# Attention over 32 graphs: transposed probabilities go between partition quadrants through a scratch tensor in HBM

## The chip, the cores and the metric

The kernel runs on one core of one Trainium2 chip. The metric is the device time of one execution in microseconds (us), the median of several runs. A core has five engines with their own instruction streams: PE (matrix multiplications; its weight loads are shown apart, as PEld), DVE (vector), ACT (scalar functions), POOL and SP. In this kernel SP does nothing but issue DMA transfers.

## The reference, cut to what matters

There are 32 graphs of 512 nodes with 256 features each (`x`), and a 512 x 512 adjacency matrix each (`adj`). Four layers follow one another, each with a residual and a layer normalization:

```
q, k, v = split_heads(x @ Wq + bq), ...              # 8 heads of 32
scores  = where(adj > 0, q @ k.T / sqrt(32), NEG)
x = layernorm(x + softmax(scores) @ v @ Wo + bo)      # layer 0
x = layernorm(x + relu(((1+eps) x + adj @ x) @ W1 + b1) @ W2 + b2)              # layer 1
x = layernorm(x + silu(rmsnorm((eps x + adj @ x) @ W1 + b1)) @ W2 + b2)         # layer 2
x = layernorm(x + softplus(xn @ W_self + (I - normalized adj) @ xn @ W_neigh))  # layer 3
```

All of it is in 32-bit floating point. The graphs are independent of each other.

## The kernel before, in words

The function `graph(b)` records the operations of one graph; nothing is issued while it runs. Each recorded operation has one or more ways, and a way names an engine, a cost in nanoseconds and the code that issues it. When all 32 graphs are recorded, `Order.emit` plays the operations through a list scheduler and issues them in the order it finds. Every engine takes, among the operations that can start within 100 ns of the earliest, the one with the lowest due time. The due time of an operation is the graph's number times `PERIOD`, plus its place in its own graph (a mix of earliest and latest, weighted by `LATE`), plus a shift for its stage from the table `LEAD`; the last graph is brought forward by `HASTE`. The scheduler also knows the number of buffers of each tile, a cost `TURN` for changing the shape in which PE's array is used[...]. So work of several graphs is interleaved, and costs, shifts and period decide the order on every engine.

Attention (`attend(g)`) works on groups of four heads and on row tiles of 128 nodes: 2 groups x 4 row tiles, eight row tiles per graph, 256 in all. For one row tile:

1. PE computes scores for four heads into the four banks of `sc` (L715, four passes side by side, each on 32 rows of the array).
2. DVE adds the mask `bias`, takes the row maximum and writes to `pq`, once per head (L734). ACT takes the exponential in place (L748).
3. DVE transposes `pq` in place (L761). Its transpose works within blocks of 32 x 32, so afterwards blocks sit in the wrong group of 32 partitions (a quadrant).
4. Sixteen DMA moves carry each 32-partition block of `pq` to its place in `pT` (L773), 64 KB each. In the first graph the moves of a tile are four operations, which the scheduler may give to SP's or ACT's queue; in the other graphs all sixteen are one operation on SP.
5. PE multiplies the values with two row tiles of `pT` into `po_att` (L815, four passes side by side, each on 32 columns of the array).

There are two `pq` buffers and three `pT` buffers. PSUM has four banks for `sc` and four more (tag `m`) that all other matrix products take turns in: `pq` of the projections (L643), `pv` (L684), `pm_t` and `pr_r` of the softmax denominators (L862, L875), `po` (L902), `ph` (L1077), `pa` and `pg` (L1094), `pm` and `pb` of the root mean square (L1180, L1210), `pt` (L1270), `pz` (L1298) and `pa_l` (L1340). The copy from `pr_r` to `oT` is at L526, the step that empties a `pz` bank into `zy` is at L1309, its scaling at L1325 or L1319. The loads of `adjT` and `xT`, in rows of 128 bytes, are at L565; `adj` and `x` have loads of their own (L390, L387).

Of the kernel before, what the change touches and what calls it, by code (L numbers as in the profile page):

```python
# [9 lines left out]
F32 = mybir.dt.float32  # L10
# [9 lines left out]
RMS_EPS = 1e-6  # L20
HEADS = 8

PERIOD = 73742
LEAD = {
    "adjT": 6800, "agg1": 6800, "agg2": -35400, "degree": -29100, "diag": -31500,
    "lap": -106500, "ln0": -12800, "ln1": -36800, "ln2": 4400, "ln3": 118000, "load": 57500,
    "move": -2300, "pv": -3300, "pz": 12100, "qk": 46700, "rinv": -33100, "rms": -12600,
    "scores": -3500, "silu": -120800, "softplus": -44300, "v": 78100, "w11": -39800,
    "w12": -64200, "w21": -29300, "w22": 4400, "wo": -14600, "x3T": -44400, "xT": -7800,
}  # L30


# [27 lines left out]
class Order:  # L60
# [8 lines left out]
    WAIT = 70  # L69
    TABLE, TABLE_DUE = 1300, 9000  # L70

    TURN = {"whole": 93, "row": 180, "col": 93}
    TURN_DUE = 4000
    LATE = 0.97
    HASTE = 53985

    def __init__(self):
        self.ops = []
# [29 lines left out]
    def run(self, ops, key, back=False):  # L108
# [20 lines left out]
        slots = {}  # L129
        cand = {e: [] for e in self.LAT}  # L130
        table, turn = [None], ["whole"]
        pool_busy = [0.0, 0.0]

        def add(o):
            for i, way in enumerate(o.ways):
# [18 lines left out]
        while len(out) < len(ops):  # L154
            best = None
            for e, lst in cand.items():
                if not lst:
                    continue
                opts = []
                for c in lst:  # L160
                    o = c[2]
                    st = slot_time(o)
                    if st is None:
                        continue
                    t = max(free[e], o.ready, st)
                    way = o.ways[c[3]]
                    if e == "DVE" and "port" in way[3] and pool_busy[0] <= t < pool_busy[1]:
                        t = pool_busy[1]
                    k = c[0]
                    tb = way[3].get("table")  # L170
                    if tb and tb != table[0]:
                        k += self.TABLE_DUE
                    if e == "PE" and way[3].get("turn", "whole") != turn[0]:
                        k += self.TURN_DUE
                    if len(o.ways) > 1:
                        f0 = t + way[1]
                        worse = False
                        for j, other in enumerate(o.ways):
                            if j != c[3] and max(free[other[0]], o.ready) + other[1] < f0 - 1:
                                worse = True  # L180
                        if worse:
# [26 lines left out]
            if e == "PE":  # L208
                tu = way[3].get("turn", "whole")
                if tu != turn[0]:  # L210
                    cost += self.TURN[tu]
                    turn[0] = tu
            if e == "POOL" and cost > 500:
                pool_busy[:] = [t, t + cost]
            for way2 in o.ways:
                lst = cand[way2[0]]
                for i in range(len(lst) - 1, -1, -1):
                    if lst[i][2] is o:
                        del lst[i]
            o.t0, o.t1, o.way = t, t + cost, way  # L220
            free[e] = o.t1 - self.TAIL[e] if e != "SP" else t + way[3].get("issue", 100)
            end = o.t1 + way[3].get("lat", self.LAT[e])
            for x in o.bufs:
                if not x.taken:
                    x.taken = True
                    s = slots[x.slot]
                    s.remove(min(s))
# [50 lines left out]
def kernel(  # L278
# [40 lines left out]

    const = ctx.enter_context(tc.tile_pool(name="const", bufs=1))  # L320
    sb = ctx.enter_context(tc.tile_pool(name="sb", bufs=2))
    ps = ctx.enter_context(tc.tile_pool(name="ps", bufs=1, space=PSUM))


# [168 lines left out]
    def graph(b):  # L493
# [74 lines left out]
        d_out, d_in = small("d_out"), small("d_in")  # L568
        for q in range(4):
            op(  # L570
                [("SP", 1650, lambda q=q: load_blocks(adjT(), adj[b], q), {"issue": 1650, "lat": 6000})],
                [], [(adjT, m, q) for m in range(NT)],
            )
        for m0 in range(0, NT, 2):
# [31 lines left out]
        xT = tmp([P, DC, N], "xT", 1)  # L606
        for q in range(4):
            op(
                [("SP", 800, lambda q=q: load_blocks(xT(), x[b], q), {"issue": 800, "lat": 4000})],
                [], [(xT, c, q) for c in range(DC)],  # L610
            )
        dve(
# [87 lines left out]
        def attend(g):  # L700
# [6 lines left out]
            for t in range(NT):  # L707
# [59 lines left out]
                pT = tmp([P, 4, HPG, NT, 32], "pT", 3)  # L767
                pTs.append(pT)

                def move(queue, to, pq=pq, pT=pT):  # L770
                    for a in to:
                        for i in range(4):
                            queue.dma_start(  # L773
                                pT[32 * a : 32 * a + 32, i], pq[32 * i : 32 * i + 32, a]
                            )

                pqk = [(pq, j) for j in range(HPG)]
                if first:

                    for a in range(4):  # L780
                        op(
                            [
                                (
                                    "SP", 2230,
                                    lambda a=a, move=move: move(nc.sync, [a]),
                                    {"issue": 2230},
                                ),
                                (
                                    "ACT", 2400,
                                    lambda a=a, move=move: move(nc.scalar, [a]),  # L790
                                    {"lat": 2000},
                                ),
                            ],
                            pqk, [(pT, a)],
                        )
                else:
                    op(
                        [(
                            "SP", 8900, lambda move=move: move(nc.sync, range(4)),
                            {"issue": 8900},  # L800
                        )],
                        pqk, [(pT, a) for a in range(4)],
                    )

                if t % 2 == 0:
                    continue
# [3 lines left out]
                def pv(two=two):  # L810
# [10 lines left out]
                            )  # L821

                pe(
                    1960, pv,
                    [(pT, a) for _, pT in two for a in range(4)] + [(v, c) for c in range(NT)],
                    [(po,)], oT, turn="col",
                )
# [3 lines left out]
            tj = [(t, j) for t in range(NT) for j in range(HPG)]  # L831
            rv = small("rv", 2, [P, NT, HPG])
            dve(
                170,
                lambda: nc.vector.reciprocal(rv(), rs()),
                [(rs, t, j) for t, j in tj], [(rv,)],
            )
# [2 lines left out]
            for r in range(3):  # L840
                dst = part[:, :, :, r]
                dve(
                    150,
                    lambda dst=dst, left=left: nc.vector.tensor_copy(dst, left()),
                    [(left,)], [("parts", g), ("parts", g, r)], port=True,
                )
                if r < 2:
                    rest = small("rest", 2, [P, NT, HPG])
                    dve(
                        150,  # L850
                        lambda dst=dst, left=left, rest=rest: nc.vector.tensor_tensor(
                            rest(), left(), dst, ALU.subtract
                        ),
# [6 lines left out]
            def tr():  # L860
# [10 lines left out]
            )  # L871
            pr_r = bank("pr_r")
            pe(
                220,
                lambda: nc.tensor.matmul(  # L875
                    pr_r(),
                    lhsT=sel_r.rearrange("p j e -> p (j e)"),
# [415 lines left out]
        for t in range(NT):  # L1293
            pz = bank("pz")

            def mm(t=t, pz=pz):
                for c in range(DC):
# [23 lines left out]
                    ),  # L1321
                ),
                (
                    590,
                    lambda t=t: nc.scalar.activation(  # L1325
                        zy[:, t, D : 2 * D], zy[:, t, D : 2 * D], AF.Identity,
                        scale=s_in[:, t : t + 1],
# [5 lines left out]
        for tp in range(NT // 2):  # L1333
            pa = bank("pa_l")
            for i in range(2):
                t = 2 * tp + i

                def mm(t=t, i=i, pa=pa):
# [6 lines left out]
                            stop=(m == NT - 1),  # L1345
                        )

                pe(1740, mm, allT + [(zy, m, 1) for m in range(NT)], [(pa, i)])
                dve(
                    430,  # L1350
                    lambda t=t, i=i, pa=pa: nc.vector.scalar_tensor_tensor(
                        out=zy[:, t, 0:D],
                        in0=pa[:, i * D : (i + 1) * D],
# [99 lines left out]
```

## Time and profile before

| | |
|---|---|
| median of 3 runs | 3562.94 us (3562.31 to 3564.2) |
| the profiled execution | 3560.7 us, span 3558.9 us |
| mean granted TensorE clock | 0.981 |
| busy share of the span | PE 96%, DVE 79%, PEld 57%, ACT 52%, POOL 24% |
| DMA moves `pT<-pq` | 4048 on SP's queue, 48 on ACT's, 64 KB each, 2.0 us to landing |
| DMA in all | 395.10 MB, 653361 packets |
| HBM | 105.79 MB read, 16.78 MB written |

The profile is that of one execution. The span runs from the first to the last instruction; the execution's own time has a little around it. Busy time of an engine is the time in which one of its instructions was running; for PE, matrix passes overlap and their ends are modelled, so 96% busy does not mean 96% of its peak. The granted clock is the share of full speed that the chip gave PE.

### The profile page before, as it was taken

To read this page: it belongs to the slowest core of one execution; us is meant where nothing else is said; L and a number is where in the kernel's file an instruction comes from. 1 tells how busy PE (TensorE), PEld (TensorE's weight loads), DVE (VectorE), ACT (ScalarE), POOL (GpSimd) and SP (SyncE) were. 2 spreads that over 40 slices of the span, in tenths; PEclk is the share of its full clock that TensorE was granted. 3 is DMA by queue.
4 is the path that set the end of the run, shared out by engine and by line. 5 is a ranking of instruction groups with operands and counts; after the bars stand their busy time and mean duration, and the time that the engine had idled before them with its cause. 6 is when DMAs were issued, how large, how long until landed. Compare 5 with 4: busy or idle time off the path is not lost.

```text
span 3558.9 us, 59695 instructions
## 1 busy us (share of the span) xinstructions
PE 3404.3 (96%) x19848; PEld 2031.2 (57%) x19848; DVE 2817.0 (79%) x6324; ACT 1865.4 (52%) x3797; POOL 863.1 (24%) x614
## 2 busy tenths in 40 slices
PE   5799999999999999999999999999999999999997
PEld 2455655655655655556565556565556556556565
DVE  5778787888787888787888877887887888788865
ACT  2355554465554555555555545555554555554633
POOL 0122222222222222221222221322221222222221
PEclk7999999999999999999999999999999999999998
DMA  6644444444444454444444444444444444444420
GB/s 165 145 118 112 113 116 110 116 118 103 117 118 113 110 118 106 113 110 118 119 114 108 118 107 118 116 116 103 116 112 115 114 110 116 114 113 109 102 51 12
DMA packets 653361, 395.10 MB, mean 111 GB/s; under 512 B 468864, under 2 KB 505088, under 8 KB 653056
## 3 DMA queue, kind: packets, MB, share of 16 engines
q1 hardware_dynamic: 650752, 388.14, 45.9%
q10 hardware_dynamic: 2304, 3.15, 0.4%
q8 instruction: 160, 2.62, 0.3%
q14 instruction: 145, 1.19, 0.1%
HBM read 105.79 MB, written 16.78 MB: 34 GB/s over the span
## 4 chain that ended last, share of the span: by engine, by line
PE 75%; SPq 12%; DMA 5%; DVE 4%; issue 2%; ACT 1%; POOL 0%; DVEq 0%; POOLq 0%; ACTq 0%
PE po L902 13%; PE pg L1094 12%; SPq L773 12%; PE ph L1077 11%; PE pa_l L1340 6%; PE po_att L815 6%; PE sc L715 6%; PE pa L1094 5%; PE pq L643 5%; PE pz L1298 4%; PE pv L684 3%; DMA pT<-pq 3%; DVE pq L734 2%; DMA x<-in_x_dram 1%; PE pm L1180 1%
## 5 line engine op out<-in xcount | busy, mean ns | idle before, releaser
L748 ACT ACTIVATE pq<-pq,mx 128x512 f32<-128x512 f32 x1024 | 727.3, 711 | 610.0 <-DVE mx L734 308.6
L734 DVE CUSTOM_DVE_ANT_0 pq<-sc,bias 128x512 f32<-128x512 f32 x1024 | 658.5, 685 | 235.1 <-DMA pT<-pq 180.7
L761 DVE STREAM_TRANSPOSE pq<-pq 128x2048 f32<-128x2048 f32 x256 | 587.9, 2297 | 85.3 <-ACT pq L748 82.6
L902 PE MATMUL po<-w,gT 128*128 128x256 f32 x2048 | 460.0, 383 | 4.3 <-ACT gT L1233 4.3
L1094 PE MATMUL pg<-hT,w 128*128 128x512 f32 x1024 | 447.8, 596 | 0.0
L955 POOL TENSOR_TENSOR rstd<-ve,nhalf 128x4 f32<-128x4 f32 x132 | 143.5, 1087 | 1226.6 <-DVE ve L950 1052.4
L902 PEld LDWEIGHTS po<-w,gT 128*128 128x128 f32 x2048 | 389.0, 191 | 82.7 <-issue 23.6
L715 PE MATMUL sc<-kT,qT 32*128 32x512 f32 x2048 | 298.9, 653 | 40.1 <-DVE mx L734 26.1
L1094 PEld LDWEIGHTS pg<-hT,w 128*128 128x128 f32 x1024 | 192.4, 190 | 252.1 <-issue 221.2
L1298 PE MATMUL pz<-wsn,xnT 128*128 128x512 f32 x512 | 259.4, 634 | 49.7 <-DVE zy L1309 28.6
L533 POOL TENSOR_TENSOR ssq<-ssq,sq 128x512 f32<-128x512 f32 x219 | 287.4, 1312 | 67.0 <-ACT sq L1170 55.6
L815 PEld LDWEIGHTS po_att<-pT,v 128*32 128x32 f32 x8192 | 224.2, 113 | 110.2 <-issue 60.9
L815 PE MATMUL po_att<-pT,v 128*32 128x128 f32 x8192 | 261.8, 281 | 16.4 <-DMA pT<-pq 12.7
L533 POOL TENSOR_TENSOR sp<-sp,y 128x1024 f32<-128x1024 f32 x31 | 73.0, 2354 | 774.1 <-ACT sp L1390 750.1
L1077 PE MATMUL ph<-adjT,y 128*128 128x512 f32 x512 | 230.6, 593 | 0.0
L1340 PE MATMUL pa_l<-zy,adjT 128*128 128x256 f32 x1024 | 229.1, 381 | 1.2 <-ACT zy L1325 0.9
L1077 PE MATMUL ph<-adjT,y_att 128*128 128x512 f32 x512 | 229.8, 601 | 0.0
L1094 PE MATMUL pa<-hT,w 128*128 128x512 f32 x512 | 228.3, 599 | 0.0
L902 PE MATMUL po<-w,aT 128*128 128x256 f32 x1024 | 226.7, 380 | 0.7 <-DVE aT L1118 0.7
L1340 PEld LDWEIGHTS pa_l<-zy,adjT 128*128 128x128 f32 x1024 | 193.5, 190 | 44.8 <-issue 14.8
L902 PEld LDWEIGHTS po<-w,aT 128*128 128x128 f32 x1024 | 192.4, 190 | 27.1 <-DVE aT L1118 1.7
L1374 ACT ACTIVATE sp<-zy 128x1024 f32<-128x1024 f32 (+1 forms) x33 | 34.0, 1031 | 319.8 <-PE ph L1077 297.7
(136 smaller groups left out, 5101.9 us busy)
## 6 DMA issues: line engine op xcount, KB each, us to landing
pT<-pq SPq DMA_DIRECT2D x4048, 64.0 KB, 2.0
adj<-in_adj_dram SPq DMA_DIRECT2D x32, 1024.0 KB, 5.3
adjT<-in_adj_dram SPq DMA_DIRECT2D x128, 256.0 KB, 4.4
xT<-in_x_dram SPq DMA_DIRECT2D x128, 128.0 KB, 3.7
x<-in_x_dram SPq DMA_DIRECT2D x32, 512.0 KB, 5.4
out_dram<-sp SPq DMA_DIRECT2D x31, 512.0 KB, 3.3
pT<-pq ACTq DMA_DIRECT2D x48, 64.0 KB, 2.2
w<-in_L_gnn_W_dram SPq DMA_DIRECT2D x2, 1024.0 KB, 6.1
```

Source lines behind the costliest of these rows:

```text
L533: lambda: nc.gpsimd.tensor_tensor(dst(), dst(), src(), ALU.add), {},
L715: nc.tensor.matmul(sc[:, j, :], lhsT=qT[hp, g, t * P : (t + 1) * P], rhs=kT[hp, g, :], start=True, stop=True,)
L734: lambda t=t, j=j, sc=sc, row=row: nc.vector.tensor_tensor_reduce(out=row(), in0=sc[:, j, :].rearrange("p (a n) -> p a n", a=4), in1=bias[ ...
L748: lambda t=t, j=j, row=row: nc.scalar.activation(row(), row(), AF.Exp, bias=mx[:, t, j : j + 1], scale=-1.0, accum_out=rs[:, t, j : j + 1],),
L761: lambda pq=pq: nc.vector.transpose(pq().rearrange("p a j c s -> p (a j c s)"), pq().rearrange("p a j c s -> p (a j c s)"),),
L773: queue.dma_start(pT[32 * a : 32 * a + 32, i], pq[32 * i : 32 * i + 32, a])
L815: nc.tensor.matmul(po[j * HD : (j + 1) * HD, t * P : (t + 1) * P], lhsT=v[:, c, h * HD : (h + 1) * HD], rhs=pT[:, :, j, c, :], start=(c == 0),
L902: nc.tensor.matmul(po[:, i * D : (i + 1) * D], lhsT=lhs[:, k, t * P : (t + 1) * P], rhs=w[:, k, :], start=(i == 0 and k == 0), stop=(i == ...
L1077: nc.tensor.matmul(ph(), lhsT=xin[:, m, c * P : (c + 1) * P], rhs=adjT[:, m, :], start=(m == 0), stop=(m == NT - 1),)
L1094: nc.tensor.matmul(pa(), lhsT=w[:, c, m * P : (m + 1) * P], rhs=hT[:, c, :], start=(c == 0), stop=(c == DC - 1),)
L1298: nc.tensor.matmul(pz(), lhsT=xnT[:, c, t * P : (t + 1) * P], rhs=wsn[:, c, :], start=(c == 0), stop=(c == DC - 1),)
L1340: nc.tensor.matmul(pa[:, i * D : (i + 1) * D], lhsT=adjT[:, m, t * P : (t + 1) * P], rhs=zy[:, m, D : 2 * D], start=(m == 0), stop=(m == N ...
```

## The change

The moves between quadrants go through HBM. A new pool `dr` holds a scratch tensor `via` with four buffers. After the transpose, four DMAs write a quadrant of `pq` each (256 KB, all four target quadrants at once); when they have landed, one DMA reads 1 MB into `pT`, where each partition's 8 KB are contiguous. All of them are on SP's queue, for the first graph too.

```diff
+    dr = ctx.enter_context(tc.tile_pool(name="dr", bufs=1, space=bass.MemoryType.DRAM))
...
-                def move(queue, to, pq=pq, pT=pT):
-                    for a in to:
-                        for i in range(4):
-                            queue.dma_start(
-                                pT[32 * a : 32 * a + 32, i], pq[32 * i : 32 * i + 32, a]
-                            )
...
-                    op(
-                        [(
-                            "SP", 8900, lambda move=move: move(nc.sync, range(4)),
-                            {"issue": 8900},
-                        )],
-                        pqk, [(pT, a) for a in range(4)],
-                    )
...
+                via = Buf(dr, [4, 32, 4, HPG * NT * 32], F32, "via", f"via_{b}", 4)
+
+                def away(pq=pq, via=via):
+                    for i in range(4):
+                        nc.sync.dma_start(
+                            via[:, :, i, :].rearrange("a p e -> p a e"),
+                            pq[32 * i : 32 * i + 32].rearrange("p a j c s -> p a (j c s)"),
+                        )
+
+                op(
+                    [("SP", 2240, away, {"issue": 2240, "lat": 4500})],
+                    [(pq, j) for j in range(HPG)], [(via,)],
+                )
+                op(
+                    [(
+                        "SP", 600,
+                        lambda pT=pT, via=via: nc.sync.dma_start(
+                            pT().rearrange("p i j c s -> p (i j c s)"),
+                            via().rearrange("a p i e -> (a p) (i e)"),
+                        ),
+                        {"issue": 600, "lat": 5500},
+                    )],
+                    [(via,)], [(pT, a) for a in range(4)],
+                )
```

The scheduler's numbers change with it: `PERIOD` from 73742 to 71815, every entry of `LEAD`, `TURN` for the row shape from 180 to 200, `TURN_DUE` from 4000 to 4750, `LATE` from 0.97 to 1.14, `HASTE` from 53985 to 24390.[...] Some costs change, among them these:

```diff
-                [("SP", 1650, lambda q=q: load_blocks(adjT(), adj[b], q), {"issue": 1650, "lat": 6000})],
+                [("SP", 1250, lambda q=q: load_blocks(adjT(), adj[b], q), {"issue": 1250, "lat": 4500})],
...
-                    1960, pv,
+                    1780, pv,
...
-                    590,
+                    500,
                     lambda t=t: nc.scalar.activation(
                         zy[:, t, D : 2 * D], zy[:, t, D : 2 * D], AF.Identity,
...
-                    430,
+                    475,
                     lambda t=t, i=i, pa=pa: nc.vector.scalar_tensor_tensor(
                         out=zy[:, t, 0:D],
```

What is computed does not change, and the instructions on PE are the same ones in another order.

More of the change, by code (lines that the diff above doesn't have):

```diff
@@ L21 @@
 HEADS = 8
-PERIOD = 73742
+PERIOD = 71815
 LEAD = {
[L25 to L29, printed above, removed]
+    "adjT": 118100, "agg1": 26800, "agg2": -178200, "degree": 63800, "diag": 700,
+    "lap": -205500, "ln0": -84700, "ln1": -132100, "ln2": -13100, "ln3": 175600, "load": 16100,
+    "move": -135200, "pv": 1100, "pz": -31400, "qk": 19100, "rinv": -44200, "rms": -37100,
+    "scores": -14700, "silu": -127000, "softplus": 8300, "v": 122200, "w11": 17900,
+    "w12": -76100, "w21": 900, "w22": 5000, "wo": -50100, "x3T": -163400, "xT": -19500,
 }
@@ L70 @@
     TABLE, TABLE_DUE = 1300, 9000
[L72 to L75, printed above, removed]
+    TURN = {"whole": 93, "row": 200, "col": 93}
+    TURN_DUE = 4750
+    LATE = 1.14
+    HASTE = 24390
     def __init__(self):
@@ L131, in run @@
         table, turn = [None], ["whole"]
-        pool_busy = [0.0, 0.0]
+        pool_busy, dve_busy = [0.0, 0.0], [0.0, 0.0]
         def add(o):
@@ L168, in run @@
                         t = pool_busy[1]
+                    if e == "POOL" and dve_busy[0] <= t < dve_busy[1]:
+                        t = dve_busy[1]
                     k = c[0]
@@ L212, in run @@
                     turn[0] = tu
-            if e == "POOL" and cost > 500:
+            if e == "POOL" and cost > 1100:
                 pool_busy[:] = [t, t + cost]
+            if e == "DVE" and "port" in way[3]:
+                dve_busy[:] = [t, t + cost]
             for way2 in o.ways:
@@ L608, in graph @@
             op(
-                [("SP", 800, lambda q=q: load_blocks(xT(), x[b], q), {"issue": 800, "lat": 4000})],
+                [("SP", 660, lambda q=q: load_blocks(xT(), x[b], q), {"issue": 660, "lat": 4000})],
                 [], [(xT, c, q) for c in range(DC)],
@@ L768, in attend @@
                 pTs.append(pT)
-                def move(queue, to, pq=pq, pT=pT):
-                    for a in to:
-                        for i in range(4):
-                            queue.dma_start(
-                                pT[32 * a : 32 * a + 32, i], pq[32 * i : 32 * i + 32, a]
-                            )
-                pqk = [(pq, j) for j in range(HPG)]
-                if first:
-                    for a in range(4):
-                        op(
[L782 to L794, printed above, removed]
-                        )
-                else:
-                    op(
-                        [(
-                            "SP", 8900, lambda move=move: move(nc.sync, range(4)),
-                            {"issue": 8900},
-                        )],
-                        pqk, [(pT, a) for a in range(4)],
-                    )
@@ L833, in attend @@
             dve(
-                170,
+                240,
                 lambda: nc.vector.reciprocal(rv(), rs()),
@@ L842, in attend @@
                 dve(
-                    150,
+                    190,
                     lambda dst=dst, left=left: nc.vector.tensor_copy(dst, left()),
@@ L849, in attend @@
                     dve(
-                        150,
+                        180,
                         lambda dst=dst, left=left, rest=rest: nc.vector.tensor_tensor(
@@ L873, in attend @@
             pe(
-                220,
+                130,
                 lambda: nc.tensor.matmul(
@@ L1346, in mm @@
                         )
-                pe(1740, mm, allT + [(zy, m, 1) for m in range(NT)], [(pa, i)])
+                pe(1728, mm, allT + [(zy, m, 1) for m in range(NT)], [(pa, i)])
                 dve(
-                    430,
+                    475,
                     lambda t=t, i=i, pa=pa: nc.vector.scalar_tensor_tensor(
```

## The prediction

> **What bounds the kernel now.** I read the page first, then the stretches, then PE's waits, then DVE's and the DMA issues, then the timeline.
>
> ```profile
> span 3558.9 us, 59695 instructions
> PE 3404.3 (96%) x19848; PEld 2031.2 (57%) x19848; DVE 2817.0 (79%) x6324; ACT 1865.4 (52%) x3797; POOL 863.1 (24%) x614
> ...
> PEclk7999999999999999999999999999999999999998
> ```
>
> PE is the bound: 96% busy, the next engine 79%. No engine but PE can shorten the middle of the run; PE can do so only by idling less, by running less often at a low clock, or by needing fewer changes of array shape. Where its idle time lies is told by four stretches (length, then busy time of PE, PEld, DVE, ACT, POOL, then clock, DMA share, GB/s):
>
> ```profile
> 0.00:120.00 120.00, 63.54 (x439) 33.30 (x440) 75.94 (x163) 38.70 (x102) 9.84 (x13) 0.76 0.72 170
> 120.00:270.00 150.00, 135.57 (x818) 76.05 (x817) 116.13 (x256) 69.32 (x146) 33.88 (x23) 0.97 0.48 120
> 270.00:3330.00 3060.00, 3004.73 (x17663) 1794.55 (x17663) 2486.74 (x5584) 1662.75 (x3396) 776.16 (x543) 0.99 0.48 113
> 3330.00:3559.00 229.00, 200.47 (x933) 127.32 (x931) 138.21 (x325) 94.60 (x154) 43.22 (x35) 0.94 0.20 49
> ```
>
> PE idles 120 - 63.5 = 56 us in the first stretch, 14 in the second, 55 in the long middle, 29 at the end. The start is a third of all idle time in 3% of the span. PE's waits in the middle alone (waiting line, what it waited for, us in total, times, longest):
>
> ```profile
> PE pz L1298 <- DVE zy L1309: 28.6, 9, 3.6
> PE pz L1298 <- ACT oT L526: 20.7, 18, 1.9
> PE sc L715 <- DVE mx L734: 4.0, 10, 1.2
> ```
>
> No line there names a DMA: the 16 moves per row tile are hidden from PE in the middle. They aren't hidden from the engines that feed it; over the whole run:
>
> ```profile
> ACT pq L748 <- DMA pT<-pq: 230.0, 52, 15.0
> DVE pq L734 <- DMA pT<-pq: 180.7, 112, 4.9
> ```
>
> These are reductions and exponentials that can't overwrite a `pq` buffer (two of them) until its 16 moves have landed. Issues (KB each, median us to landing):
>
> ```profile
> pT<-pq SPq DMA_DIRECT2D x4048, 64.0 KB, 2.0
> adj<-in_adj_dram SPq DMA_DIRECT2D x32, 1024.0 KB, 5.3
> ...
> out_dram<-sp SPq DMA_DIRECT2D x31, 512.0 KB, 3.3
> ```
>
> What one change of array shape costs, from the timeline:
>
> ```profile
> 1502.79 3.62 PE L902 MATMUL po<-wo,oT 128*128 128x256 f32 x16
> 1506.24 7.07 PE L902 MATMUL po<-w,gT 128*128 128x256 f32 x32
> 1513.24 1.14 PE L715 MATMUL sc<-kT,qT 32*128 32x512 f32 x8
> 1514.31 7.17 PE L902 MATMUL po<-w,gT 128*128 128x256 f32 x32
> 1521.42 1.14 PE L715 MATMUL sc<-kT,qT 32*128 32x512 f32 x8
> ```
>
> From start to start 16 passes take 3.45 us, so 32 take 6.90; between two score groups they take 7.11. The score group takes 1.07 for two rounds of four passes side by side, 0.86 at 0.43 a pass. The detour adds 0.21 + 0.21 us for two changes: **0.21 us a change**.
>
> **What the Trainium skill says.** "TensorEngine Tiling (Array Packing)", Key Properties: changing the tiling mode drains TensorE; the 0.21 us agree. "TensorE: Matmul & The Clock Gate", Part 1: the clock falls to half after an idle window of about 3.4 us and needs a busy one to recover. The trace agrees: after the 3.6 us wait at 799 us, four `pz` passes take 3.5 us instead of 1.8. So a long stall costs about 1.7 us more than its length; the short ones aren't followed by this. "DMA: Bandwidth & Descriptors", Anatomy of one DMA: a fixed 2 us, mostly the receipt of the write, heaviest for HBM, plus bytes / 436 GB/s. That fit (it is for the gpsimd path) gives an estimate of 2.6 us for 256 KB and 4.4 us for 1 MB; the trace's 512 KB store takes 3.3, its 1 MB load 5.3, slower than the fit.
>
> **The change part by part.**
>
> *SP's issue time.* Before: 16 x 0.589 us (median of L773) = 9.4 us per row tile, 75 us per graph of about 107. After: four writes at the same price and one read at 0.53 (the `adj` load): 2.9 us per tile, 23 per graph. SP wasn't PE's bound, so this alone is worth nothing in the middle.
>
> *Latency of one tile.* Before 9.4 + 2.0 = 11.4 us. After: 4 x 0.589 to issue, a landing W of the last write, 0.5 to issue the read, a landing R. No row shows a 256 KB write to HBM from 32 partitions; W lies between 2.1 us (fastest store to the output) and 3.4 (slowest), I take 2.7. R is a 1 MB load: 4.4 (skill) to 10 (slowest `adj` load), I take 5.3. Sum 2.4 + 2.7 + 0.5 + 5.3 = 10.9 us, 9.4 to 16.3. No gain here; but `pq` is free after 2.4 + 2.7 = **5.1 us instead of 11.4**, and four scratch buffers stand between `pq` and the three `pT`.
>
> *Start.* A `pq` buffer's cycle is 2.7 us of reductions, 0.9 of the last exponential, 2.3 of transpose, then the move: 17.3 us before, 8.7 per tile with two buffers; the first 11 score groups start 10.2 us apart (16.7 to 118.5 us). After, 11.0 / 2 = 5.5. Then DVE is next: its 76 us in the first 120 are about 6.6 per tile. 11 tiles at 8 instead of 10.2 save 24 us. DMA limits it: share 0.72 already, and 12 reads of 1 MB are added at about 3 us of all engines each (358 GB/s below): (0.72 x 120 + 36) = 122 us of DMA work in the same stretch, unless the order spreads it, which it does in part, since weights move later. The first graph also loses ACT's queue for moves. I take **-20 us**, bounds -45 (DVE alone) and +5.
>
> *Order in the middle.* `PERIOD`, `LEAD`, `LATE` and the costs reorder every engine. Several costs come to what the trace shows: L1351 from 430 to 475 (trace 472), L1325 from 590 to 500 (498). In PE's order the four `pz` groups of a graph, split by other shapes before, follow each other behind 6.9 us of `po`, so DVE has emptied `xnT` and their banks by then; and three score groups stand 6.9 us apart, which the old 8.7 us cycle couldn't have fed and 5.5 can. The waits shown are 53 of 55 us idle, plus 9 long ones x 1.7 = 15 us at low clock: 70 us at stake. PE's producers DVE and ACT keep their load (the order moves some 55 `gT` copies from DVE to ACT, and others back). I take **-45 us**, bounds -70 and +10.
>
> *Changes of shape.* Counting PE's order by 128x128, 32-row and 32-column groups: 727 before, 675 after. 52 x 0.21 = **-11 us**.
>
> *New waits.* The read waits on SP for its write to land and for a `pT`; behind it on SP stand the next writes and loads, so a late `po_att` holds them. Four `po_att` groups now stand within some 30 us, around the eight `pg`. With three `pT`, the read of the last of these tiles can start only when the first half of the third group is done; from there to the second half of the fourth PE has 0.9 + 1.1 (`sc`) + 0.9 (`pm`) + 3.5 (`pq`) + 0.9 (`pb`) + 1.0 = **8.3 us** of other work. The read needs 0.5 + 5.3 = 5.8 if the rings are empty. They aren't: in those 30 us, five reads, one or two tiles of writes, an `adj` load and the end of `adjT` want the engines. The `adj` load shows the price of a load with long rows:
>
> ```profile
> 1500.00:1504.00 4.00, 4.00 (x46) 3.47 (x47) 2.92 (x5) 3.83 (x4) 0.00 (x0) 1.00 0.64 229
> ```
>
> 229 GB/s at a share of 0.64 is 358 GB/s in full, 2.9 us per MB; moves alone ran at 103 GB/s for 0.42, 4.3 us per MB. Five reads 15, two tiles 9, `adj` 3: 27 of 30 us. Over the run 256 x 2.9 us add 0.21 to a share of 0.46. I take **+15 us** (0.5 us a graph), bounds 0 and +130.
>
> *End.* The tail after the last `pg` has the same matmuls with little moved: 0, bounds -5 and +5.
>
> Sum: -20 - 45 - 11 + 15 = -61 us. The profiled execution took 3560.7 us (span 3558.9), 2.2 under the median 3562.9, which is nothing against these bounds. Predicted: 3502 us.
>
> **The rivals.** *A, reads late at `po_att`*: for it, 27 of 30 us; against it, no DMA wait of PE in the middle today. If they land 3 us past their slack at two groups a graph, PE waits 2 x 3 us, 31 times: +186, less 76 gained: 3670. It decides from 76 / 31 = 2.5 us of new PE waiting per graph on. *B, start and shape changes alone*: the new order has waits of its own in place of those at `pz` (DVE is 79% busy and in order): -20 - 11 = 3531. *C, both work out*: no stall left in the middle, DVE alone at the start: -45 - 70 - 11: 3436. *D, nothing*: moves were hidden and new waits eat the rest: 3563.
>
> **How the numbers follow.** About 0.2% (7 us) is what a measurement of this kernel can tell from no change. Forecast (3480 to 3520) 0.45, B 0.16, C 0.14, D 0.05 within 0.2%, slower 0.20 (A 0.14, a wait of DVE's in the new order 0.06). Faster 0.75. The range of 8 in 10 leaves out most of A and the lower end of C: 3435 to 3590.
>
> **What would show it.** Right: PE idle in the first 120 us near 35; `pz` gone from PE's waits; DMA waits of L734 and L748 far smaller; DMA share near 0.67; SP's queue mostly idle. Wrong: `po_att` behind `DMA pT<-via` at the top of PE's waits, each graph; a read landing over 8 us; a mean clock below 0.981.

## The result, and the profile after

The change makes the kernel 0.3% faster: **3551.5 us** (median of 17 runs) against 3560.4 us (17 runs), ratio 0.9971, 95% interval 0.9959 to 0.9983. The sign of the forecast was right and its size was not: about 9 us came of 61. The profiled execution took 3558.9 us, at the slow end of its runs, and its span is only 2.3 us shorter than that of before; the gains and losses below are told against the spans.

The heads of the page of after, to set beside those of before:

```profile
span 3556.6 us, 55212 instructions
PE 3393.6 (95%) x19848; PEld 2032.6 (57%) x19848; DVE 2823.1 (79%) x6308; ACT 1900.1 (53%) x3810; POOL 839.8 (24%) x613
```

PE is busy for 10.7 us less, but the span shrank by 2.3 only: idle time grew by 8.4. The same four stretches tell where (length, busy time of PE, PEld, DVE, ACT, POOL, clock, DMA share, GB/s):

```profile
0.00:120.00 120.00, 64.90 (x362) 30.49 (x362) 67.00 (x140) 37.15 (x92) 8.37 (x12) 0.76 0.90 235
120.00:270.00 150.00, 133.78 (x892) 77.98 (x893) 116.97 (x265) 72.44 (x163) 30.82 (x22) 0.95 0.73 224
270.00:3330.00 3060.00, 2990.49 (x17614) 1792.17 (x17616) 2495.21 (x5561) 1696.80 (x3399) 758.75 (x545) 0.99 0.68 190
3330.00:3557.00 227.00, 204.45 (x990) 131.98 (x982) 143.91 (x343) 93.74 (x156) 41.89 (x34) 0.96 0.31 86
```

PE's idle time, before to after: 56.5 to 55.1 us in the first 120 us, 14.4 to 16.2 in the next 150, **55.3 to 69.5 in the middle**, 28.5 to 22.6 at the end. The loss is in the middle. PE's waits there (waiting line, what it waited for, us in total, times, longest):

```profile
PE pb L1207 <- DVE diag L1201: 50.8, 27, 4.4
PE sc L721 <- DVE mx L740: 9.1, 5, 2.1
PE pz L1295 <- DVE y L913: 4.4, 8, 1.7
...
PE po_att L812 <- DMA pT<-via: 0.3, 1, 0.3
```

The waits at `pz` are gone, as forecast (49.3 us before, 4.4 now), and the read of the scratch tensor is never late for `po_att`. But `pb`, the product that spreads the root mean square over the partitions in layer 2, waits once in nearly every graph. No DMA is named, so one has to ask why `diag` was late. The timeline of one graph, on all engines (start, length, engine, line, operation; in brackets the idle time before it and what ended it):

```profile
1382.02 0.38 SPq L396 DMA_DIRECT2D adj<-in_adj_dram  x1
...
1389.15 1.05 PE L1177 MATMUL pm<-ones,ssq 128*128 128x1 f32 x8
...
1390.89 2.29 DVE L1001 TENSOR_REDUCE d_in<-adj 128x4 f32<-128x2048 f32 x1 [2.10 <-DMA adj<-in_adj_dram]
...
1393.10 0.15 DVE L1189 TENSOR_SCALAR ms<-pm 128x4 f32<-128x4 f32 x1
...
1393.33 1.02 POOL L549 TENSOR_TENSOR rr<-ms,nhalf 128x4 f32<-128x4 f32 x1 [5.40 <-DVE ms L1189]
...
1394.38 0.87 DVE L1201 TENSOR_SCALAR diag<-ident,rr 128x128 f32<-128x128 f32 x4
...
1395.40 1.10 PE L1207 MATMUL pb<-diag,ones 128*128 128x512 f32 x2 [1.65 <-DVE diag L1201]
```

Read it from below. `pb` waits for `diag`, `diag` for POOL's `rr`, `rr` for `ms`. The input of `ms`, the sums in `pm`, was ready at 1390.2 while DVE stood still, yet `ms` starts at 1393.1: on DVE it stands behind `d_in`, the row sum of the next graph's adjacency matrix, and here DVE keeps to its order. `d_in` stood still for 2.1 us because its load, issued at 1382.0, took 8.8 us to arrive. Over the whole run:

```profile
DVE pq L740 <- DMA via<-pq: 72.4, 45, 8.4
DVE d_in L1001 <- DMA adj<-in_adj_dram: 70.6, 28, 5.7
```

The first line is the gain that was sought: reductions waited 180.7 us for the moves, now 72.4 for the writes (ACT's exponentials 230.0 before, 3.9 now). The second is new. The DMA issues of the page show why (KB each, median us from issue to landing):

```profile
via<-pq SPq DMA_DIRECT2D x1024, 256.0 KB, 4.4
pT<-via SPq DMA_DIRECT2D x256, 1024.0 KB, 7.6
adj<-in_adj_dram SPq DMA_DIRECT2D x32, 1024.0 KB, 8.8
...
out_dram<-sp SPq DMA_DIRECT2D x31, 512.0 KB, 7.2
```

The load of `adj` takes 8.8 us instead of 5.3, in a middle whose DMA share has gone from 0.48 to 0.68.

That it matters is due to the new order as well. In the kernel before, `d_in` started some 30 us after its load was issued; one graph of it:

```profile
1385.64 0.53 SPq L390 DMA_DIRECT2D adj<-in_adj_dram  x1
...
1416.19 2.27 DVE L1004 TENSOR_REDUCE d_in<-adj 128x4 f32<-128x2048 f32 x1
```

A load of 8.8 us would have been in time there. After the change DVE comes to `d_in` 6.8 us after the issue (at 1388.8 in the graph above), and in 26 of the 32 graphs the next instruction on DVE is `ms`. The scheduler of both kernels counts 6.0 us for this load (4000 ns of its own, at L562 of the kernel after, and 2000 of `LAT`); by that number there was no wait to see.

### The profile page after: what moved, and what is told of

Read it like the earlier page. It is cut to its first block, busy times and chain, and to the rows that moved or that the text cites. A ratio compares the mean times of both kernels' runs of the same rounds, so it can differ in the third digit from the quotient of the medians.

```text
span 3556.6 us, 55212 instructions
## 1 busy us (share of the span) xinstructions
PE 3393.6 (95%) x19848; PEld 2032.6 (57%) x19848; DVE 2823.1 (79%) x6308; ACT 1900.1 (53%) x3810; POOL 839.8 (24%) x613
## 4 chain that ended last, share of the span: by engine, by line
PE 67%; DMA 14%; DVE 11%; SPq 4%; issue 2%; ACT 1%; POOL 0%; DVEq 0%; POOLq 0%; ACTq 0%
PE po L899 15%; PE ph L1074 10%; PE pg L1091 9%; PE pa_l L1337 6%; PE pz L1295 6%; PE sc L721 5%; DMA adj<-in_adj_dram 5%; PE po_att L812 5%; DMA via<-pq 5%; PE pa L1091 4%; PE pv L690 3%; DVE pq L767 3%; DVE pq L740 3%; DMA xT<-in_x_dram 2%; SPq L571 2%
## 5 line engine op out<-in xcount | busy, mean ns | idle before, releaser
L740 DVE CUSTOM_DVE_ANT_0 pq<-sc,bias 128x512 f32<-128x512 f32 x1024 | 661.6, 683 | 88.5 <-DMA via<-pq 72.4
L1091 PE MATMUL pg<-hT,w 128*128 128x512 f32 x1024 | 458.5, 601 | 3.4 <-DVE gT L1146 2.8
L952 POOL TENSOR_TENSOR rstd<-ve,nhalf 128x4 f32<-128x4 f32 (+1 forms) x132 | 131.1, 994 | 1290.0 <-DVE ve L947 1234.7
L1295 PE MATMUL pz<-wsn,xnT 128*128 128x512 f32 x512 | 232.1, 603 | 5.6 <-DVE y L913 4.4
```

The source lines that it names most:

```text
L740: lambda t=t, j=j, sc=sc, row=row: nc.vector.tensor_tensor_reduce(out=row(), in0=sc[:, j, :].rearrange("p (a n) -> p a n", a=4), in1=bias[ ...
L952: lambda: nc.gpsimd.tensor_tensor(rstd[:, part], ve[:, part], nhalf[:, part], ALU.pow),
L1091: nc.tensor.matmul(pa(), lhsT=w[:, c, m * P : (m + 1) * P], rhs=hT[:, c, :], start=(c == 0), stop=(c == DC - 1),)
L1295: nc.tensor.matmul(pz(), lhsT=xnT[:, c, t * P : (t + 1) * P], rhs=wsn[:, c, :], start=(c == 0), stop=(c == DC - 1),)
```

## The experiments

Line numbers differ by some ten to twenty between kernels. Ratios are to the kernel before, which ran on the same chip each time.

### e1_din_later: take `d_in` out of the way

After the scheduler has found its order, 26 of the 32 row sums are put behind the next `diag` on DVE; no other engine's order is touched.

```diff
         out = self.run(self.ops, lambda o: keys[o.n])
+        is_din = lambda o: o.stage == "degree" and o.way[0] == "DVE" and o.way[1] == 2300
+        is_spread = lambda o: o.stage == "rms" and o.way[0] == "DVE" and o.way[1] == 880
+        for d in [o for o in out if is_din(o)]:
+            i = out.index(d)
+            for k in range(i + 1, min(i + 60, len(out))):
+                if d in out[k].succs or d.n in out[k].preds:
+                    break
+                if is_spread(out[k]):
+                    out.insert(k, out.pop(i))
+                    break
```

> The changed kernel with one instruction per graph moved on DVE: the degree sum (L1001 in the profile after), which waits for the adj load of the next graph, comes after the four instructions that make diag for pb instead of ahead of ms. PE's and SP's orders stay. Theory 1 (DVE stands in line behind a late adj load, 8.8 us to landing instead of 5.3, and holds up ms, diag and so pb): PE's wait at pb falls from 50.8 us to under 10, DVE's wait for adj shrinks to under 20 or is hidden, time about 3551 - 45 = 3505 (ratio to before about 0.984). Theory 2 (pb is late because the order leaves only 3.5 us of PE work between pm and pb, whatever stands ahead of ms): at least half of the wait stays, time above 3530.

Measured: **3484.9 us, ratio 0.979 (0.9768 to 0.9812)**, 67 us below after by the medians (64 by the ratios). Its page, its middle stretch and PE's waits in that stretch:

```profile
PE 3369.3 (97%) x19848; PEld 2021.0 (58%) x19848; DVE 2820.6 (81%) x6308; ACT 1900.5 (55%) x3810; POOL 839.5 (24%) x613
...
adj<-in_adj_dram SPq DMA_DIRECT2D x32, 1024.0 KB, 8.5
```

```profile
270.00:3250.00 2980.00, 2960.18 (x17543) 1776.16 (x17542) 2486.96 (x5553) 1696.93 (x3399) 758.38 (x545) 1.00 0.69 195
```

```profile
PE sc L731 <- DVE mx L750: 9.5, 5, 2.2
PE pg L1101 <- DVE gT L1156: 3.5, 2, 1.8
PE pz L1305 <- DVE y L923: 3.0, 5, 0.9
...
PE pb L1217 <- DVE diag L1211: 0.7, 1, 0.7
```

The load still lands late, 8.5 us, but DVE now waits for it 8.0 us in all and `pb` 0.7. PE idles 20 us in the middle instead of 69.5. The span is 77.2 us shorter than after's: PE idles 52.9 us less in all and is busy 24.3 us less for the same passes in the same order. The mean granted clock rose from 0.982 to 0.988; the span times what is missing from 1 gives 64 and 42 us lost, an estimate, so most of the 24.3 us is low clock. Theory 1 had given 3505 us; it had left this term out.

So one position in DVE's order held what the change had gained. What made it costly was this order and the late load together: in the graph above `pb` waits 0.45 us less than `d_in`, and of the 26 waits of `d_in` right ahead of `ms` only one is longer than 3.5 us (4.9). With a landing 3.5 us earlier, as in before, 1 or 2 of the 50.8 us would be left. That is an estimate; no run has this order with an early load.

### e5_one_more_transfer: the dose doubled

After each scratch read, SP also copies the same 1 MB to a second scratch tensor, which nobody reads. The DMA engines move 395 MB in before, 663 in after and 932 here. SP has 256 transfers more to issue and the scratch buffers are held for longer, so it isn't a dose of DMA load alone.

```diff
+                    more = dr.tile([P, 4 * HPG * NT * 32], F32, tag="more", name="more", bufs=4)
+                    nc.sync.dma_start(more, via().rearrange("a p i e -> (a p) (i e)"))
```

> The changed kernel with one transfer more per row tile: after each scratch read 1 MB is copied from the scratch tensor to another place in HBM, which nobody reads. Theory 1 (what the change costs in the middle is the load on the DMA engines, which makes adj late): adj lands 2 to 4 us later than 8.8, PE's wait at pb doubles to 100 us or more, waits at po_att appear in the middle, slower than the changed kernel by 60 us or more. Theory 2 (the engines had room at a share of 0.68): share near 0.85, adj within 1 us of 8.8, time within 20 us of the changed kernel.

Measured: 4057.0 us, ratio 1.1408 (1.1386 to 1.1431), 505 us above after by the medians. The issues of its page, and PE's waits in its middle:

```profile
pT<-via SPq DMA_DIRECT2D x256, 1024.0 KB, 8.8
adj<-in_adj_dram SPq DMA_DIRECT2D x32, 1024.0 KB, 14.5
```

```profile
PE pb L1208 <- DVE diag L1202: 151.4, 27, 9.1
PE po_att L813 <- DMA pT<-via: 91.9, 27, 4.9
PE sc L721 <- DVE mx L740: 80.9, 52, 2.5
```

With the load at 14.5 us, more than the 2 to 4 us later that were expected, `pb` waits three times as long, at the same 27 places: the dose and the response belong together. Only now is the read late at `po_att` in the middle, once a graph, which is what the prediction's rival A had described (0.3 us in after).

### e7_adj_on_act_queue: a queue of its own for the load

```diff
-        nc.sync.dma_start(t(), adj[b].rearrange("(t p) j -> p t j", p=P))
+        queue = nc.scalar if b > 2 else nc.sync
+        queue.dma_start(t(), adj[b].rearrange("(t p) j -> p t j", p=P))
```

> The changed kernel (the degree sum in its old place ahead of ms) with the adj load of graphs 3 to 31 issued by ACT instead of SP, at the same place of the program; it then has a queue of its own instead of standing behind two 1 MB scratch reads. Theory 1 (adj is late because it stands behind those reads in one queue): it lands in under 7 us instead of 8.8, DVE's wait for it falls from 70.6 us to under 30, PE's at pb from 50.8 to under 25, time 20 to 50 us under the changed kernel's 3551. Theory 2 (it is late because the engines' time is shared, whatever the queue): it lands in over 8 us, with the waits of the changed kernel, time within 8 us of it or above, ACT losing a little to the wait for the adj buffer.

Measured: 3557.3 us, ratio 1.0008 (0.9988 to 1.0029), no better than after. Its issue of the load, and PE's first wait in its middle:

```profile
adj<-in_adj_dram ACTq DMA_DIRECT2D x29, 1024.0 KB, 8.8
```

```profile
PE pb L1208 <- DVE diag L1202: 61.2, 27, 6.2
```

8.8 us again: that the load is issued by SP, among reads and writes, isn't what makes it late. "DMA: Bandwidth & Descriptors" of the Trainium skill, section "Issuing engines are not separate DMA queues", says that transfers run on the same 16 DMA engines and interleave there, whichever engine started them; the run agrees, 8.8 us on either queue.

### e3_old_numbers_scratch and e4_new_numbers_moves: the two halves of the change

e3 has the scratch transport with the scheduler's numbers, costs and rules of before; e4 the 16 moves with those of after, the new rule on when POOL may start (`dve_busy`) included. The scheduler plans anew for each, so neither has the exact order of before or after.

```diff
-PERIOD = 71815
+PERIOD = 73742
...
-    LATE = 1.14
-    HASTE = 24390
+    LATE = 0.97
+    HASTE = 53985
```

> The kernel before with the scratch tensor alone: all of the scheduler's numbers and costs are the old ones but those of the two new operations. Theory 1 (in the middle the moves were hidden already, so the way through HBM brings nothing by itself; what moves PE is the order and what then comes late): within 25 us of the kernel before on either side, PE's waits in the middle of the same total as before, 40 to 80 us, with the start no shorter than 50 us of idle time. Theory 2 (the pq buffers that come free after 5 instead of 11 us are worth something under any numbers): over 20 us faster than before, with under 30 us of PE waits in the middle.

> The changed kernel with the 16 moves in place of the scratch tensor, under the new numbers. Theory 1 (the new order needs the pq buffers early: three score groups stand 6.9 us apart, and a buffer's cycle with moves allows 8.7 us): PE waits for DVE at the scores or for pT at po_att, over 60 us in the middle, slower than before by 20 us or more; the adj load lands in 5 to 6 us. Theory 2 (the numbers carry the gain and the moves are as good): 10 to 50 us faster than before, with pb's wait gone since adj lands early.

| | old numbers | new numbers |
|---|---|---|
| 16 moves | 3560 (before) | **3722** (e4, ratio 1.0454, 1.0434 to 1.0473) |
| scratch | **3530** (e3, ratio 0.9911, 0.989 to 0.9931) | 3552 (after), 3485 with `d_in` later (e1) |

With the old numbers the scratch is worth 31 us; the new numbers cost the moves 162 us. The 31 us aren't idle time: PE idles 153.3 us in e3 and 154.6 in before, but is busy 28.6 us less, at a mean granted clock of 0.987 against 0.981 (by the estimate used at e1, 22 us of it). Neither theory of e3 fits whole: the gain is beyond the 25 us of the first, and the waits in the middle, some 60 us, beyond the 30 of the second. PE's waits in the middle of e3, then of e4, and of e4's DVE over the whole run:

```profile
PE po L893 <- ACT v L527: 28.6, 28, 1.0
PE po_att L806 <- DMA pT<-via: 25.4, 23, 2.0
```

```profile
PE pt L1276 <- DVE oT L530: 61.2, 26, 3.5
PE po_att L821 <- DMA pT<-pq: 44.9, 29, 2.8
```

```profile
DVE pq L739 <- DMA pT<-pq: 292.7, 114, 4.5
```

In e3 the load of `adj` lands nearly as late (8.1 us), but DVE waits for it 1.9 us in the whole run: in that order `d_in` comes late enough. So a late load alone costs nothing; a late load and an early `d_in` do. In e4 the reductions wait 292.7 us for the moves, 180.7 in before; that fits the prediction's argument that the new numbers count on the short cycle of `pq`, but doesn't show it. The load lands in 6.4 us there, so most of its lateness comes with the scratch, and a part with the numbers (5.3 and 6.4 with moves, 8.1 and 8.8 with the scratch). In e4 `d_in` starts some 29 us behind the issue of its load (1439.9 and 1468.8 us in one graph), so it doesn't tell what after's order would do with an early one.

### The start: six kernels built on e1

The forecast gain in the first 120 us didn't come, so six kernels vary the start of e1, which idles 55.3 us in its first 120 and 13.5 in the next 150.

**e6_weights_later**: the four large weight loads, 3 MB, go behind the sixth scratch read on SP.

```diff
+        heavy = [o for o in out if o.b < 0 and o.way[0] == "SP" and o.way[1] > 1000]
...
+        out[k:k] = heavy
```

> The kernel of e1 with the four large weight loads (3 MB, about 9 us of all DMA engines) moved on SP's queue behind the sixth scratch read; nothing else moves. Theory 1 (the start is as slow as before because its transfers fill the DMA engines, share 0.90 in the first 120 us): the first scratch tiles land earlier, PE's waits at po_att in the first 150 us fall from 30 us to under 20, and the time is 5 to 12 us under e1. Theory 2 (the start is set by the order and by DVE's and SP's queues, not by the transfers' volume): within 4 us of e1, with the same waits at po_att.

Measured: 0.9809 (0.9788 to 0.9829), 7 us above e1, with intervals that overlap. PE idles 62.8 us in the first 120, and a projection waits 9.2 us for `xT`, which is new; `po_att` waits for reads as long as in e1 over the first 270 us (29.6 against 29.4). It doesn't tell the theories apart.

**e8_write_before_read**: in the first two graphs each read goes behind the next tile's writes, so that SP doesn't stand still at the read.

```diff
+        for d in [o for o in out if is_back(o) and o.b <= 1]:
...
+                    out.insert(k, out.pop(i))
```

> The kernel of e1 in which, for the first two graphs alone, each scratch read stands on SP's queue one write later (behind the writes of the next row tile, where nothing that needs the read comes between). Other engines' orders stay. Theory 1 (the start is slow because SP is in order: a read waits about 7 us for its own writes to land, and the next tile's writes, which need no such wait, stand behind it, so that a tile takes 9.3 us): PE's idle time in the first 150 us falls by 10 us or more, time 8 to 20 us under e1. Theory 2 (the volume of transfers sets the start, share 0.88): within 4 us of e1. Theory 3 (po_att needs each read early and PE stands in line behind it): slower than e1.

Measured: 0.9839 (0.9818 to 0.9861), 17 us above e1 by the ratios, as its third theory says. The later reads make `po_att` wait twice as long, 61.5 us against 29.4 in the first 270 us.

**e9_first_graph_moves** and **e10_two_graphs_moves**: the first one or two graphs use the 16 moves again, all on SP, in the same order.

```diff
+                        if first:
+                            for a in range(4):
+                                nc.sync.dma_start(
+                                    pT[32 * a : 32 * a + 32, i], pq[32 * i : 32 * i + 32, a]
+                                )
+                            continue
```

> The kernel of e1 with the 16 direct moves in place of the way through HBM for the eight row tiles of the first graph, at the place of the writes on SP's queue; all orders stay. Theory 1 (the start is held by the round trip: about 7 us for a write to land, then the read, while the engines are 0.88 full): without it PE's idle time in the first 150 us falls by 8 us or more and the time is 5 to 15 us under e1. Theory 2 (SP's 9.4 us of issue per tile are as long as the round trip): within 5 us of e1.

> As e9, for the first two graphs (16 row tiles). Theory 1: another 3 to 10 us under e9. Theory 2 (16 moves take SP's queue and hold up what stands behind them): the second graph's tiles come later, 5 us or more above e9.

Measured: 0.9818 (0.9802 to 0.9833) and 0.9931 (0.9913 to 0.9949), 10 and 50 us above e1 by the ratios; the interval of e9 overlaps that of e1, the other doesn't. In e9 the DMA share of the first 120 us falls from 0.88 to 0.66 and PE idles 65 us there instead of 55. So volume alone doesn't set the start, and by e10 the scratch is the better way there too, in this order.

**e11_adjT_later** and **e12_columns_on_act** ask whether SP's queue sets it. The timeline of SP's queue in e1 shows what made me ask:

```profile
38.34 8.17 SPq L581 DMA_DIRECT2D adjT<-in_adj_dram  x2
46.61 3.90 SPq L791 DMA_DIRECT2D via<-pq  x4
50.55 1.21 SPq L803 DMA_DIRECT2D pT<-via  x1
51.87 7.78 SPq L581 DMA_DIRECT2D xT<-in_x_dram  x4
```

The second number is the time that SP was occupied issuing. It has no pause of more than 0.11 us from 38.3 to 59.7 us: two loads of `adjT`, in rows of 128 bytes, take 8.2 us to issue (the median over this run is 1.4 us each), and the writes and the read stand behind them. e11 moves the second graph's `adjT` loads behind the eighth read; e12 gives the first graph's `adjT` and the second's `xT` to ACT's queue.

```diff
+        late = [o for o in out if o.b == 1 and o.stage == "adjT" and o.way[0] == "SP"]
...
+        out[k:k] = late
```

```diff
+            queue = nc.scalar if (b, kind) in ((0, "adjT"), (1, "xT")) else nc.sync
+            queue.dma_start(dst[32 * q : 32 * q + 32].rearrange("r m (i c) -> r m i c", c=32), v[q])
```

> e1_din_later's kernel with the four adjT loads of the second graph (256 KB each, in rows of 128 bytes; SP issues them from 73 to 90 us there, in 10.8 us, and their transposes on DVE start at 132 us) moved on SP behind the eighth scratch read (119.5 us). Theory 1 (what sets the start is SP's queue: column loads stand ahead of writes and reads, and while the DMA engines are behind, each takes up to 4 us to issue instead of 1.3): PE's idle time of the first 120 us falls from 55 to 45 us or less, the fourth and fifth po_att wait 8 us less, and the whole run is 5 to 12 us below e1's 0.979, if the transposes at 132 us don't wait. Theory 2 (the DMA engines' time sets it, or DVE's chain): idle stays at 52 to 58 us, and the ratio within 0.002 of 0.979, or it is above because the loads come late for DVE.

> e1_din_later's kernel with the adjT loads of the first graph and the xT loads of the second issued by ACT instead of SP: about 18 us of SP's issue time of the first 92 us go to ACT, which is busy 37 of the first 120 us there. Theory 1 (SP's queue sets the start): the scratch reads of tiles three and four are issued 5 to 8 us earlier, PE's idle time of the first 120 us falls from 55 to 47 us or less, the ratio is 0.975 to 0.978. Theory 2 (the DMA engines' time sets it): the loads take ACT as long to issue as they took SP, exponentials stand behind them, idle time of the first 120 us stays or grows by up to 15 us, ratio 0.979 to 0.985.

Measured: e11 0.9777 (0.9753 to 0.9801), the same as e1; e12 **3473.2 us, 0.9758 (0.9739 to 0.9777)**, the fastest kernel of this study, though its interval touches that of e1. The first two stretches of e1, e11 and e12, in this order:

```profile
0.00:120.00 120.00, 64.71 (x362) 31.16 (x362) 67.64 (x141) 37.03 (x92) 8.36 (x12) 0.76 0.88 236
120.00:270.00 150.00, 136.50 (x906) 79.96 (x907) 118.87 (x271) 72.77 (x164) 30.84 (x22) 0.97 0.74 228
```

```profile
0.00:120.00 120.00, 70.17 (x444) 35.29 (x444) 72.80 (x151) 40.11 (x100) 8.38 (x12) 0.79 0.88 244
120.00:270.00 150.00, 131.24 (x815) 76.38 (x815) 111.64 (x255) 69.65 (x155) 30.84 (x22) 0.94 0.72 219
```

```profile
0.00:120.00 120.00, 69.72 (x438) 34.52 (x439) 72.85 (x151) 40.35 (x100) 8.37 (x12) 0.77 0.90 253
120.00:270.00 150.00, 139.52 (x858) 80.37 (x857) 120.72 (x278) 73.02 (x162) 34.29 (x24) 0.98 0.73 226
```

Both gain 5 us of PE time in the first stretch. e11 gives them back in the second (-5.3), where its loads now fall and a new wait of `po` for DVE stands (7.4 us; that the loads cause it wasn't shown); e12 keeps them and gains 3 more. Idle time of the first 120 us came to 50.3 us in e12, not the 47 or less that theory 1 asked for. SP's queue is a part of what sets the start; the larger part stays open. The same section of the Trainium skill says that issuing from several engines saves only issue time, usually small beside the transfer; in this start it was about 8 us of PE's idle time over the two stretches (68.8 to 60.8).

## Why the prediction was right and wrong

- **Order in the middle, -45 us: the step that failed.** The half about `pz` was right (49.3 us of waits became 4.4). But a wait at `pb` took their place, 50.8 us, and the middle idles 14.2 us more than before. In its mechanism this was the prediction's rival B, waits of the new order in place of those at `pz`, given 0.16; its 3531 us counted on the start, so the measured time lies beyond it, towards rival D. (A wait of DVE's in the new order also stood among the slower outcomes, at 0.06, with no place named.) The working missed it in one place: it counted the load of `adj` among the traffic around the reads (27 of 30 us) and asked who waits for the reads, but not who waits for `adj`, nor how soon after its issue. The order of DVE, where `d_in` stands ahead of `ms`, was there to be read before the result.
- **New waits, +15 us, at `po_att`: wrong place.** The contention was sized well (share of the run forecast at 0.67, measured 0.66), and the read landed in 7.6 us instead of 5.3. Yet in the middle `po_att` waited 0.3 us; late reads stood in the start. In the middle the same contention came out at another transfer, with 51 us of waits and low clock on top.
- **Start, -20 us: no gain in sum.** PE idles 1.4 us less in the first 120 us and 1.8 more in the next 150. What was sought came there: PE's waits for the row maxima fell from 16.2 to 4.8 us. But its waits at `po_att`, 6.7 us for the moves, became 23.0 for the reads. The working had found 122 us of DMA work in these 120 us, and still took 8 us a tile, a figure that it doesn't derive. W, the landing of a write, was put at 2.7 us; it is 4.4 over the run and 6.5 in the first 150 us. So a `pq` buffer is free after some 9 us there, not 5.1. SP's queue did become mostly idle over the run (occupied 36% of it, 79% in before), but it is occupied without a pause for 21 us of the start (e1); what e12 saved by taking some of that off SP, 8 us of idle time, is two fifths of the forecast gain.
- **Changes of shape, -11 us: agrees.** PE is busy 10.7 us less with the same passes. The mean granted clock is 0.981 and 0.982, by the estimate used at e1 a difference of some 4 us, so this isn't a measurement of that term alone.
- **Low clock: mis-sized.** The prediction held that only long stalls are followed by it. "TensorE: Matmul & The Clock Gate" of the Trainium skill, Part 1, puts the idle window at about 3.4 us, as cited there; the traces have it behind shorter waits, of 1.86 us at `pz` in before (2303 us) and of 1.95 us at `pb` in after (2253 us). Taking the waits away in e1 cut busy time by 24.3 us besides 52.9 of idle time.
- **End, 0:** 28.5 to 22.6 us of idle time, just beyond its bound of 5.
- **The sum.** Start +0.4, middle +14.2, end -5.9, busy time -10.7: -2.0, against -2.3 in the span. With `d_in` moved, e1 is 79.5 us below before by the spans (44.5 of idle time, 35.0 of busy time), more than the -61 of the forecast. The gain was there; one wait took it.

## What to carry to other kernels

When a change adds DMA traffic, list every load that gets slower, not only the new ones, and for each find the instruction that waits for it, how long after the issue it comes (30 us before, 7 after), and what stands behind it on its engine; the price is paid by whatever stands there, even if it has nothing to do with the load. After a change of this size, look for the new top line among the bound engine's waits and follow it back to the first thing that was late: here moving one instruction a few places back on DVE was worth some seven times the change itself (67 us against 9, by the medians). And numbers tuned for an order (period, shifts, costs) belong to the transport that they were tuned with: with the other one they cost 162 us here.

## What the runs showed of the hardware

- Landing times grew with the traffic, and not alike. From a run's share of 0.46 (before) over 0.66 (after) to 0.72 (e5) the 1 MB load of `adj` took 5.3, 8.8 and 14.5 us; the write of 256 KB hardly moved between the last two (4.4 and 4.5), the read of 1 MB a little (7.6 and 8.8). The share doesn't set it alone: in e4, at 0.43, the load of `adj` took 6.4 us. And the scratch adds to what HBM reads and writes as well (106 and 17 MB in before, 374 and 285 in after); no run tells whether HBM or the DMA engines make the load late.
- Issuing isn't a fixed price either: a load of `adjT`, in rows of 128 bytes, took SP 0.6 us at best and 1.5 in the median of after, and 7.0 at most in e1's crowded start.
- A wait of about 2 us may or may not be followed by a low clock. Two lines of after's timeline for the same 64 passes, each behind a `pb` that had waited 2.2 us (2.21 at 1502 us, 2.23 at 2687 us):

```profile
1502.93 1.95 PE L812 MATMUL po_att<-pT,v 128*32 128x128 f32 x64
```

```profile
2688.40 3.38 PE L812 MATMUL po_att<-pT,v 128*32 128x128 f32 x64
```

The second takes 1.4 us longer; the granted clock was 1.00 from 1502.9 to 1505 us and 0.56 from 2688.4 to 2691.8. Why one wait is followed by it and its equal isn't, no run here tells.
